# Two-layer graph network: five of the seven products of q, k and v at quarter size, instruction order from tables

## Chip, core and metric

The kernel runs on one core of a Trainium2 chip. The metric is the device time of one execution in microseconds. All data is float32. The core has a matrix engine (TensorE, PE in the profile, with PEld for its weight loads), a vector engine (DVE), an activation engine (ACT), GpSimd (POOL) and a queue that issues transfers (SP). Each of these works through a list of instructions; instructions of different engines are tied together by semaphores. Matrix products are written into eight PSUM banks, from which DVE and ACT take them to SBUF.

## The reference

Two layers over 64 graphs of 256 nodes with 512 features: a graph convolution, then an attention with 8 heads of 64. Cut to what matters:

```python
# x: (64, 256, 512), adj: (256, 256)
h = jnp.maximum(_layernorm(x, axis=-1), 0.0)
x = x + (jnp.einsum('nm,bmd->bnd', adj, h) @ weight + bias)

h = jnp.maximum(_layernorm(x, axis=-1), 0.0)
q = (h @ Wq + bq).reshape(b, n, 8, 64)
k = (h @ Wk + bk).reshape(b, n, 8, 64)
v = (h @ Wv + bv).reshape(b, n, 8, 64)
scores = jnp.einsum('bqhd,bkhd->bhqk', q, k) / 8.0
scores = scores + (1.0 - adj)[None, None, :, :] * -1000000000.0
attn = jax.nn.softmax(scores, axis=-1)
out = jnp.einsum('bhqk,bkhd->bqhd', attn, v).reshape(b, n, d)
x = x + (out @ Wo + bo)
```

The output is x, of shape (64, 256, 512).

## The kernel before

**Groups and layers.** The 64 graphs are taken two at a time: NG = 32 groups of GB = 2. Layer 0 runs over all groups and leaves the residual and the normalised features (transposed) in DRAM. Then layer 1 runs over the groups again. For group g its loop does: attention of the first half of the heads (`attend(g, 0)`), the scores of the second half (`score(g, 1)`), q and k of group g+1 (`queries_keys`), attention of the second half (`attend(g, 1)`), the scores of the first half of group g+1 (`score(g + 1, 0)`), v of group g+1 (`values`), and the output projection of group g (`post`). The o of the last two groups is drawn out at the end.

**Seven products for eight.** Each projection is a 512 by 512 product cut into 2 by 2 blocks, done with seven block products by Strassen's scheme in Winograd's form. With the letters that the change uses: A = a11*b11, B = s3*t3, C = a12*b21, D = a22*t4, E = s4*b22, F = s2*t2, G = s1*t1, where s1 to s4 are sums of weight blocks (`weight_sums`) and t1 to t4 sums of feature blocks (class `Halves`, line 433, written by POOL or DVE at line 450). A, F, G and E are added up in one PSUM bank, pa, from which the four quadrants of the result are taken in between; B and D are added up in pc. A product at the outer level (`product`, line 452) is four instructions with 128 by 128 weights and 256 columns.

**Quarter size.** From group 2 on (FIRST2 = 2) `project2` (line 545) does C, D and E once more by the same scheme: seven instructions with 128 columns each in place of four with 256 (line 568). Their inner sums of features come from the class `Blocks` (lines 541 to 543): three instructions for a Blocks object. Four of the seven (a11*b11, s2*t2, s3*t3, s1*t1 of the inner level) run through a small shared bank: a running total in its first half, which DVE (line 669) or ACT adds into the result after each step, before the next product goes on top of it, and s3*t3 in its second half. The other three go straight into the outer bank. The weights' inner sums are made once by `block_sums` on POOL.

**Order of work.** Each engine runs its instructions in the order in which the program emits them. A counter spreads side work: `after(delay, fn)` enters a piece of work, and `tick()` emits all that has fallen due, by due time and then by entry. The projections are generators; `run` calls `tick()` at each of their yields, seven for a projection. Side work that matters here: the exponentials of a score (line 1009, ACT), the key sums (line 1016, POOL), the sums t1 to t4 of the features of the group after next (`hidden_sums`), their inner sums (`block_hidden`), and the division of the attention (line 1070, DVE). `score` emits 32 matmuls into score banks (line 986), eight DVE instructions that scale and mask them (lines 994 and 997), and for the later two of its four batches a POOL subtraction of the row maximum of the mask (line 1004). Ahead of its matmuls it seeds four banks by ACT (line 259) and emits the inversion of the attention's denominators (lines 1048 to 1052, ACT and POOL).

**Where the inner sums of the features are emitted before.** When v of group g+1 has been emitted, the loop calls `hidden_sums(g + 2, 2, 3, 4, 5)` and `block_hidden(g + 2, 6)`, and then runs o of group g with its seven ticks: the four t sums fall due at ticks 2 to 5, the inner sums of both graphs (`both.sums`) at 6 and those of t4 (`last.sums`) at 7.

**Banks.** `bank()` takes the first free bank of a list (one that holds fresh data everywhere where a seed is to be written, preferably one that does not where `partial` is given) and `give()` puts it at the end.

**Buffers.** `xpool` has four buffers of 1 MB that rotate: in layer 1 for the features of two groups (H1T) and the residuals (X).

Of the kernel before, what the change touches and what calls it, by code (L numbers as in the profile page):

```python
# [196 lines left out]

@with_exitstack
def kernel(
# [37 lines left out]
    xpool = main.enter_context(tc.tile_pool(name="x", bufs=4))  # L237
# [11 lines left out]
    def bank(shape, name, seed=None, times=1.0, partial=False):  # L249

        if seed is not None:
            i = next(i for i in free_banks if whole[i])
        else:
            i = next((i for i in free_banks if not (partial and whole[i])), free_banks[0])
        free_banks.remove(i)
        t = psum.tile(shape, F32, tag=f"bank{i}", name=name)
        bank_of[id(t)] = (i, t)
        if seed is not None:
            nc.scalar.mul(t, seed, times)  # L259
        return t  # L260
# [34 lines left out]
    def load(g):  # L295
        X[g] = xpool.tile([P, T, D], F32, tag="x", name=f"x_{g}")
        for k in range(GB):
            for i in range(NI):
                nc.sync.dma_start(blocks_of(X[g], i, k), by_block(x[g * GB + k], i))
# [133 lines left out]
    class Halves:  # L433

        def __init__(self, name, tokens, which):
            self.tokens = tokens
            self.t = {n: act.tile([P, 2, N], F32, tag=f"{n}{which}", name=f"{n}_{name}")
                      for n in ("t1", "t2", "t3", "t4")}
# [72 lines left out]
    ONCE = {"a12": "b21", "a22": "t4", "s4": "b22"}  # L511
# [3 lines left out]
    def block_sums(n):  # L515

        todo = []
        for a in ONCE:
            w = W[n][a]
# [3 lines left out]
            W2[n, a] = dict(a11=part(0, 0), a12=part(0, 1), a22=part(1, 1), s1=s1, s2=s2, s3=part(1, 0), s4=s4)  # L523
            for o, p, q, op in ((s1, part(1, 0), part(1, 1), ALU.add), (s2, s1, part(0, 0), ALU.subtract),
                                (part(1, 0), part(0, 0), part(1, 0), ALU.subtract), (s4, part(0, 1), s2, ALU.subtract)):
                todo.append((nc.gpsimd.tensor_tensor, o, p, q, op))
        return todo

    class Blocks:

        def __init__(self, x, t):
            self.x, self.t = x, t

# [11 lines left out]
    def project2(n, halves, blocks, by_token, name, place, first, done=None, seeds=(), add_up=False):  # L545

        s = W[n]
# [7 lines left out]
        class Inner:  # L557

            def __init__(self, a, i, k, own, shared):
                self.w, self.x, self.own, self.shared = W2[n, a], blocks[ONCE[a]], own, shared  # L560
                self.sum, self.r = shared[:, 0:1, :], shared[:, 1:2, :]
                self.o = place(i, k)

            def mm(self, o, a, b, start=False):
                lhs, rhs = self.w[a], self.x.operand(b)
                if by_token:
                    lhs, rhs = rhs, lhs
                nc.tensor.matmul(o[:, 0, :], lhs, rhs, start=start, stop=True, skip_group_check=True)  # L568

            def begin(self, src, i, k):  # L570
                first(part(self.o, i, k), src, 0, None if by_token else i)

            def add(self, src, i, k):
                o = part(self.o, i, k)
                add(o, src if src.shape[1] == o.shape[1] else src.to_broadcast([P, o.shape[1], P]), o)

            def u1(self):
                self.mm(self.sum, "a11", "b11", True)

            def only(self, *quarters, fresh=False):  # L580
                for q in quarters:
                    a, b = {(0, 0): ("a12", "b21"), (0, 1): ("s4", "b22"), (1, 0): ("a22", "t4")}[q]
                    self.mm(part(self.own, *q), a, b, fresh)
                    fresh = False

            def u2(self):
                self.mm(self.sum, "s2", "t2")

            def s3t3(self):
                self.mm(self.r, "s3", "t3")  # L590

            def u3(self):
                self.mm(self.sum, "s1", "t1")

        def put(ps, i, k):
            first(place(i, k), ps, i)

        def more(ps, i, k):
            o = place(i, k)
            add(o, ps, o)  # L600

        def complete(i, k):
            if done:
                done(i, k)

        pa, pc = seeds or (bank([P, 2, N], f"{name}a"), None)
        product(pa, s, "a11", halves, "b11", by_token, start=not seeds, stop=False)
        put(pa, 0, 0)
        yield
        pc = pc or bank([P, 2, N], f"{name}c")  # L610
        product(pc, s, "s3", halves, "t3", by_token, start=not seeds, stop=False)
        put(pc, 1, 1)
        yield
        product(pa, s, "s2", halves, "t2", by_token, start=False, stop=False)
        put(pa, 1, 0)
        yield
        inner = []
        for a, i, k, own in (("a12", 0, 0, None), ("a22", 1, 0, pc), ("s4", 0, 1, pa)):
            inner.append(Inner(a, i, k, own, bank([P, 2, P], f"{name}{i}{k}", partial=True)))
            inner[-1].u1()  # L620
        p2, p4, p3 = inner
        for p in inner:
            if p is not p3 or add_up:
                p.add(p.sum, 0, 0)
            else:
                p3.begin(p3.sum, 0, 0)
        p2.own = pb = bank([P, 2, N], f"{name}b", partial=True)
        p2.only((0, 0), (0, 1), (1, 0), fresh=True)

        for m, n in ((0, N), (1, P)) if add_up else ((slice(0, 3), P),):  # L630
            o, u = (t if add_up else t.rearrange("p m (h j) -> p (m h) j", j=P) for t in (p2.o, pb))
            add(o[:, m, 0:n], u[:, m, 0:n], o[:, m, 0:n])
        give(pb, False)
        yield
        product(pa, s, "s1", halves, "t1", by_token, start=False, stop=False)
        more(pa, 1, 1)
        complete(1, 1)
        yield
        for p in inner:
            p.u2()  # L640
            p.s3t3()
            if p is not p3 or add_up:
                p.add(p.sum, 1, 0)
                p.add(p.r, 1, None)
            else:
                p3.begin(p3.sum, 1, 0)
                p3.begin(p3.r, 1, 1)
                p3.add(p3.r, 1, 0)
        yield
        p4.only((0, 0), (0, 1), (1, 0))  # L650
        p3.only((0, 1), (0, 0), (1, 0))
        more(pc, 1, 0)
        give(pc)
        if add_up:
            more(pa, 0, 1)
        else:
            p3.begin(part(pa, 0, 1), 0, 1)
            p3.add(part(pa, 0, 0), 0, 0)
            p3.add(part(pa, 1, None), 1, None)
        give(pa)  # L660
        for p, c in zip(inner, ((0, 0), (1, 0), (0, 1))):
            p.u3()
            p.add(p.sum, None, 1)
            give(p.shared, False)
            complete(*c)
        yield
# [193 lines left out]
    def load_hidden(g):  # L860
        H1T[g] = xpool.tile([P, GB, DC, N], F32, tag="x", name=f"h1T_{g}")
# [4 lines left out]
    def load_residual(g):  # L866
        X[g] = xpool.tile([P, T, D], F32, tag="x", name=f"x1_{g}")
        nc.sync.dma_start(X[g], X1[g].rearrange("k (t p) d -> p (k t) d", p=P))

    def hidden_sums(g, *steps):  # L870

        HH[g] = Halves(f"h_{g}", [H1T[g][:, k] for k in range(GB)], 0 if g else 1)
        for step, n in zip(steps, ("t3", "t1", "t2", "t4")):
# [3 lines left out]

    def block_hidden(g, step):

        t = act.tile([P, GB, 4, P], F32, tag="t2", name=f"t2_{g}")  # L880
        t4 = act.tile([P, 4, P], F32, tag="t24", name=f"t24_{g}")
        x = H1T[g][:, :, 2:4, :].rearrange("p k c (n j) -> p k c n j", j=P)
        H2[g] = block_sums_of(x, t, HH[g], t4, nc.gpsimd, step)

    def block_outputs(g, eng, step):
# [4 lines left out]
        else:  # L890
            t4 = act.tile([P, 4, P], F32, tag="t24", name=f"t24o_{g}")
            t = act.tile([P, GB, 4, P], F32, tag="t2", name=f"t2o_{g}")
        O2[g] = block_sums_of(x, t, HO[g], t4, eng, step)

    def block_sums_of(x, t, halves, t4, eng, step):
        both = Blocks(x, t)
        last = Blocks(halves.t["t4"].rearrange("p c (n j) -> p c n j", j=P), t4)
        after(step, both.sums, eng)
        after(step + 1, last.sums, eng)
        return {"b21": Blocks(x[:, 0], t[:, 0]), "b22": Blocks(x[:, 1], t[:, 1]), "t4": last}  # L900

    def queries_keys(g):

        for n, store in (("q", Q), ("k", K)):
            store[g] = {}
            bias = L1[n][1]

            def first(o, ps, i, m=None):
                for c in range(2) if m is None else (m,):
                    to, src = (o[:, c, :], ps[:, c, :]) if m is None else (o, ps)  # L910
                    nc.scalar.activation(to, src, AF.Identity, bias=bias[:, 2 * i + c:2 * i + c + 1])

            def place(i, k):
# [4 lines left out]
            if g < FIRST2:  # L918
                yield from project(W[n], HH[g], False, f"{n}_{g}", place, first)
            else:  # L920
                yield from project2(n, HH[g], H2[g], False, f"{n}_{g}", place, first)

    def values(g):
# [3 lines left out]
        def first(o, ps, i, m=None):  # L927
            nc.scalar.copy(o, ps)

        def place(i, k):  # L930
            return V[g][i, k]

        if g < FIRST2:
            yield from project(W["v"], HH.pop(g), True, f"v_{g}", place, first)
        else:
# [307 lines left out]
```

## Time and profile before

| | us |
|---|---|
| median of 3 runs | 2659.88 (2659.43 to 2661.59) |
| profiled execution, its own time | 2660.27 |
| its span in the trace | 2658.5 |
| scores (line 986) on PE | 240.2 in 2048 records |
| attention (line 1032) on PE | 233.6 in 4096 records |
| key sums (line 1016) on POOL | 319.6 in 256, 1.275 each |
| mask subtractions (line 1004) on POOL | 292.7 in 125, 2.363 each |
| POOL idle before the inversion (line 1050), for ACT | 452.8 in all |

A float32 matmul leaves two records on PE, so an instruction is two of the records that the profile counts. Times of records overlap, since matmuls are pipelined: what an instruction costs is read from the distance of starts. A line that ends in x8 is eight records in a row, and the number behind "idle" in a timeline is the time in which the engine stood still ahead of the instruction, with what ended it.

### The profile page before, as it was taken

How to read it: one execution, taken by the hardware profiler on the slowest of the kernel's cores; microseconds unless marked ns; L12 is line 12 of the kernel's file. 1: busy time of each engine (PE TensorE's matmuls, PEld its weight loads, DVE VectorE, ACT ScalarE, POOL GpSimd, SP SyncE). 2: the span in 40 equal slices, each digit the busy share in tenths (PEclk: the TensorE clock that was granted, in tenths of full speed). 3: DMA queues.
4: the chain of work that ended last, by engine and by line, in shares of the span. 5: the costliest groups of instructions: out<-in, count | busy, mean ns of one | idle time of the engine just before them, and what ended most of it. 6: DMA issues, size and time to landing. Idle time of an engine off the chain costs nothing. (4 is left out here: it accounts for less than half of the span.)

```text
span 2658.5 us, 52085 instructions
## 1 busy us (share of the span) xinstructions
PE 2623.4 (99%) x20076; PEld 2283.1 (86%) x20076; DVE 1648.6 (62%) x3613; ACT 1144.4 (43%) x2194; POOL 1883.9 (71%) x1899
## 2 busy tenths in 40 slices
PE   7999999999999999999999999999999999999997
PEld 6999899998888888888888888888888888888886
DVE  5878888884355555556556555556556555555556
ACT  3445454443344444444444444444444444444442
POOL 5888888774677776666677777777777776666665
PEclk9999999999999999999999999999999999999999
DMA  5776666665022211111111111111222211111110
GB/s 135 200 192 188 171 167 171 178 157 125 28 62 54 51 48 49 49 49 49 49 49 48 49 48 49 49 49 49 60 63 64 55 49 49 49 48 49 49 49 34
DMA packets 281068, 211.06 MB, mean 79 GB/s; under 512 B 145904, under 2 KB 212976, under 8 KB 280816
## 3 DMA queue, kind: packets, MB, share of 16 engines
q1 hardware_dynamic: 280352, 207.15, 29.9%
q8 instruction: 161, 2.64, 0.4%
q14 instruction: 91, 0.75, 0.1%
q10 hardware_dynamic: 464, 0.52, 0.1%
HBM read 106.96 MB, written 100.66 MB: 78 GB/s over the span
## 5 line engine op out<-in xcount | busy, mean ns | idle before, releaser
L1050 POOL TENSOR_TENSOR rest<-rest 128x512 f32<-128x512 f32 x63 | 80.1, 1271 | 452.8 <-ACT rest L1049 452.8
L1016 POOL TENSOR_TENSOR as<-a 128x512 f32<-128x512 f32 x256 | 319.6, 1275 | 57.4 <-ACT a L1009 57.4
L1004 POOL TENSOR_TENSOR a<-a,top 128x1024 f32<-128x1024 f32 x125 | 292.7, 2363 | 57.2 <-DVE a L997 57.2
L994 DVE SCALAR_TENSOR_TENSOR a<-sc,top 128x512 f32<-128x512 f32 x256 | 159.1, 684 | 276.4 <-PE sc L986 276.3
L1009 ACT ACTIVATE a<-a 128x1024 f32<-128x1024 f32 x256 | 270.8, 1059 | 4.3 <-DVE a L1002 3.1
L986 PE MATMUL sc<-q,k 64*128 64x256 f32 x2048 | 240.2, 383 | 1.4 <-ACT sc L259 1.4
L986 PEld LDWEIGHTS sc<-q,k 64*128 64x128 f32 x2048 | 196.9, 186 | 45.3 <-ACT rest L1048 25.9
L1032 PE MATMUL pav<-a,v 128*32 128x256 f32 x4096 | 233.6, 379 | 0.0
L1041 ACT ACTIVATE rest<-pden 128x512 f32<-128x512 f32 x64 | 38.2, 597 | 413.9 <-PE pden L1025 413.9
L1032 PEld LDWEIGHTS pav<-a,v 128*32 128x32 f32 x4096 | 133.3, 110 | 88.0
L42 DVE BATCH_NORM_STATS2 st<-x 128x6 f32<-128x512 f32 x256 | 173.1, 676 | 10.7 <-DMA x<-in_x_dram 8.5
L669 DVE TENSOR_TENSOR k<-k,k 128x128 f32<-128x128 f32 (+1 forms) x300 | 96.1, 353 | 126.5 <-PE k L568 124.1
L997 DVE SCALAR_TENSOR_TENSOR a<-sc,maskT 128x512 f32<-128x512 f32 x256 | 158.3, 680 | 0.0
L259 ACT ACTIVATE sc<-maskT 128x512 f32<-128x512 f32 x256 | 137.5, 591 | 0.0
L669 DVE TENSOR_TENSOR q<-q,q 128x128 f32<-128x128 f32 (+1 forms) x300 | 96.2, 353 | 65.9 <-PE q L568 63.5
L669 DVE TENSOR_TENSOR v<-v,v 128x128 f32<-128x128 f32 (+1 forms) x300 | 95.5, 351 | 65.2 <-PE v L568 62.1
L697 ACT ACTIVATE h<-x,nb,rs 128x512 f32<-128x512 f32 x128 | 93.9, 803 | 75.8 <-POOL nb L54 73.4
L824 ACT ACTIVATE h<-x,nb,rs 128x512 f32<-128x512 f32 x128 | 97.2, 807 | 52.3 <-POOL nb L54 49.1
L669 DVE TENSOR_TENSOR x<-o,x 128x128 f32<-128x128 f32 (+1 forms) x360 | 111.0, 350 | 3.1
L758 POOL TENSOR_TENSOR hs<-h 128x512 f32<-128x512 f32 x31 | 39.3, 1269 | 73.8 <-ACT h L697 63.7
L450 POOL TENSOR_TENSOR t_o<-oT,t_o 128x512 f32<-128x512 f32 x62 | 79.1, 1276 | 13.0 <-DVE t_o L450 10.6
L450 POOL TENSOR_TENSOR t_y<-yT 128x512 f32<-128x512 f32 (+1 forms) x65 | 82.2, 1265 | 5.9 <-ACT yT L808 5.9
(4817 smaller groups left out, 7302.6 us busy)
## 6 DMA issues: line engine op xcount, KB each, us to landing
x<-in_x_dram SPq DMA_DIRECT2D x256, 128.0 KB, 3.0
residual<-x SPq DMA_DIRECT2D x256, 128.0 KB, 2.5
hidden<-r SPq DMA_DIRECT2D x128, 256.0 KB, 4.5
h1T<-hidden SPq DMA_DIRECT2D x64, 512.0 KB, 9.6
x<-residual SPq DMA_DIRECT2D x32, 1024.0 KB, 7.6
out_dram<-x SPq DMA_DIRECT2D x62, 512.0 KB, 4.0
w_sb<-in_L_gnn_weight_dram SPq DMA_DIRECT2D x1, 1024.0 KB, 8.2
wq_sb<-in_L_gnn_Wq_dram SPq DMA_DIRECT2D x1, 1024.0 KB, 7.9
```

The lines of the kernel that those rows point to most:

```text
L42: nc.vector.bn_stats(st, src)
L259: nc.scalar.mul(t, seed, times)
L450: eng.tensor_tensor(self.t[n][:, c, :], self.operand(p, c), self.operand(q, c), op=ALU.subtract)
L669: nc.vector.tensor_tensor(o, ps, u, op=ALU.add)
L824: nc.scalar.activation(h1[:, k * NT + t, :], xt[:, k * NT + t, :], AF.Relu, bias=nb[:, t:t + 1], scale=rs[:, t:t + 1])
L986: nc.tensor.matmul(ps[j][:, kt * N:(kt + 1) * N], k[j * HD:(j + 1) * HD, c, kt * P:(kt + 1) * P], q[j * HD:(j + 1) * HD, c, :], start=(kt ...
L994: nc.vector.scalar_tensor_tensor(o, ps[j].rearrange("p (k n) -> p k n", k=NT), SCALE, top_b[:, 0:NT, :], op0=ALU.mult, op1=ALU.subtract)
L997: nc.vector.scalar_tensor_tensor(o.rearrange("p k n -> p (k n)"), ps[j], SCALE, maskT_f, op0=ALU.mult, op1=ALU.add)
L1004: nc.gpsimd.tensor_tensor(a, a, top_b, op=ALU.subtract)
L1009: nc.scalar.activation(a, a, AF.Exp)
L1016: nc.gpsimd.tensor_tensor(AS[c, b], a4[:, :, 0, :], a4[:, :, 1, :], op=ALU.add)
L1032: nc.tensor.matmul(po[f][h * 32:(h + 1) * 32, b * N:(b + 1) * N], v[:, k, h * HD + f * 32:h * HD + f * 32 + 32], A[h // 2, b][:, (h % 2) * ...
```

## The change

F and G join C, D and E for q, k and v: five of their seven products are now done at quarter size. o keeps C, D and E. F and G cannot add their inner sums into the four result quadrants, as they belong into the running total pa. So the running totals are copied from the small bank to a staging tile in SBUF by ACT, three copies a product (`staged`: b, e and g), DVE adds s3*t3 (h), the three direct products go into pa (i, j, k), and DVE adds the whole staging tile into pa (l).

`project2` goes away. `quartered` builds a dictionary of named steps, one for each instruction or so, and `follow` emits them in the order of a table, where "|" is a yield (a tick) and "x" the next exponential of the score before. A token is the projection (q, k, v, o), the product (A to G) and a letter or number; p and m are the takings of a quadrant from pa or pc, and z is a seed. QK interleaves q and k, VO interleaves v of group g+1 and o of group g, and V1, O1 and OL are for v or o alone: V1 in the turns of g = 1 and g = 30, O1 and OL for the o of the last two groups.

Further parts: the inner sums of the features now cover t1, t2 and t4 (`last` is a Blocks object over all three at once, in a tile kept in the fourth buffer of xpool); t3 is written over b12 (in layer 0 too); the sums of the group after next are entered by `multiplied`, when the last matmul of v has been emitted, with delays 1 to 4, 5 and 6; exponentials of the scores between the tables are not entered with a delay but taken by "x", with the key sum one tick later; the buffers of xpool have fixed tags, so the residual has one (x2), and its load is entered four ticks later; the inner sums of the weights for F and G are made on DVE, k's at ticks 16 and on in group 0.

The tables that the loop uses for most groups, and the core of the diff:

```diff
+QK = (
+    "kFa qA0 kFb qFa kGa qFb qA1 x qA2 | qGa kFc kFd kA0 kFe x kA1 | kFf kA2 kFg qA3 kFh kA3 qp000 | qFc qp001 "
+    "qFd qDa kp000 qB0 qFe qB1 kp001 | x qB2 kFl qFf qFi qFj qFg qFk qGb kB0 qFh | kB1 qFl x qGc qGd kB2 qGe kDa "
+    "kGb | qp100 kFi qGf qp101 kGc kGd qGg kFj qDb kGe kFk qGh qB3 | kp100 qGl qDc kp101 qDd qCi qp110 qDe qCj "
+    "kDb qCk qp111 qDf kGi | kGj qCl kDc kDd qGi kDe qGj kDf qGk kEa qm11 | kGk kEb kGf kDg kGg qDi kDh kEc kEd "
+    "kGh qDj kEe kGl qCa | kCa kEf kB3 qCb kCb qDg kEf2 kp110 qCc qDh qCd kp111 kEg | qCe kCc qCf kCd qEa km11 "
+    "kDi qEb qCg kDj kCe qCh kDk | qEc kCf kEi km10 qEd kEj qEe kCi kCj qEf kCk | kCg qEf2 qDk kCl qEi qEj kCh "
+    "qEk qm10 qEg qEl0 kEk | kEl1 qEh kEl0 qEl1 qEl2 kEl2 kEh ")
+VO = (
+    "vFa oBz vA0 vFb vA1 oAz vFc vFd x vGa | vA2 vB0 vGb vB1 vFe x vB2 | vFf vGc vEa vFg vGd vEb vA3 vFh vGe oA0 "
+    "| vp00 vEc vGf vCa vFl vGg vDa oA1 x vCb vGh | oA2 oA3 vFi op00 vCc vCd vEd | vCe vFj x vCf vFk vCi vCj vCk "
+    "vCg vp10 vCl oB0 | vEe oB1 vCh vEf vDb vGi vEf2 oB2 vGl vDc vDd | vB3 vDe vDf oCa vp11 oCi oCb vGj vGk vDg | "
+    "vm11 vDi vDj vDk vDh oCj oCk vm10 vEi vEj oCl0 | vEk oDa vEl0 vEg oCl1 oF0 vEl1 vEl2 oF1 vEh oF2 | oEa oF3 "
+    "oEb oB3 op10 oEc | oEd oDb oCc op11 oCd oG0 oCe oG1 oCf oEe oG2 | oEf oG3 oDi om11 oDc oDd oEg | oDe oCg oDf "
+    "oDj oDk oEh oEi oCh oEj oEk om10 oDg | oEl oDh ")
...
-                      for n in ("t1", "t2", "t3", "t4")}
+            self.all = act.tile([P, 3, 2, N], F32, tag=f"t{which}", name=f"t_{name}")
+            self.t = {n: self.all[:, i] for i, n in enumerate(("t1", "t2", "t4"))}
+            self.t["t3"] = self.operand("b12")
...
+    SMALL = {"q": "CDEFG", "k": "CDEFG", "v": "CDEFG", "o": "CDE"}
...
+        def sums(x, names):
+            t = x + "s"
+            for name, a, b, i in zip(names, ("a11", "s2", "s3", "s1"), ("b11", "t2", "t3", "t1"), (0, 0, 1, 0)):
+                multiply(x, name, a, b, t, i, None, dict(partial=True) if a == "a11" else None)
+            return t, lambda: banks[t][:, 0:1, :], lambda: banks[t][:, 1:2, :]
+
+        def staged(x, b):
+
+            t, total, rest = sums(x, "acdf")
+            held = {}
+
+            def copy(name, c):
+                def todo():
+                    if not held:
+                        held[0] = act.tile([P, 2, 2, P], F32, tag="stage", name=f"{n}_{g}_{x}", bufs=2)
+                    o = held[0][:, c[0], c[1], :] if len(c) == 2 else held[0][:, :, 1, :]
+                    nc.scalar.copy(o, total()[:, 0, :] if len(c) == 2 else total().to_broadcast([P, 2, P]))
+                step(x + name, todo, t)
+
+            def add_rest():
+                o = held[0][:, 1]
+                add(o, rest().to_broadcast([P, 2, P]), o)
+
+            def add_all():
+                u = held[0].rearrange("p k i j -> p i k j") if by_token else held[0]
+                o = banks[b].rearrange("p m (h j) -> p m h j", j=P)
+                add(o, o, u)
+            copy("b", (0, 0))
+            copy("e", (1, 0))
+            copy("g", (1,))
+            step(x + "h", add_rest, t)
+            last_three(x, "ijk", b)
+            step(x + "l", add_all, b)
+
+        def added(x, to, quadrant=None, begin=False):
+
+            t, total, rest = sums(x, "acdg")
+
+            def put_in(name, src, i, k):
+                step(x + name, lambda: first(part(to(), i, k), src(), quadrant[0], i), t, quadrant=quadrant)
+
+            def add_in(name, src, i, k):
+                def todo():
+                    o = part(to(), i, k)
+                    add(o, like(o, src()), o)
+                step(x + name, todo, t, quadrant=quadrant)
+            if begin:
+                put_in("b", total, 0, 0)
+                put_in("e", total, 1, 0)
+                put_in("f", rest, 1, 1)
+                add_in("f2", rest, 1, 0)
             else:
...
+                add_in("b", total, 0, 0)
+                add_in("e", total, 1, 0)
+                add_in("f", rest, 1, None)
+            add_in("h", total, None, 1)
...
+        product("A", "pa", True)
+        put("p00", "pa", 0, 0)
+        product("B", "pc", True)
+        put("p11", "pc", 1, 1)
+        for x, name, end, i in (("F", "p10", put, 0), ("G", "m11", more, 1)):
+            if x in SMALL[n]:
+                staged(x, "pa")
+            else:
+                product(x, "pa", False)
+            end(name, "pa", 1, i)
...
+    def follow(steps, order):
+
+        for token in order.split():
+            if token == "|":
+                yield
+            elif token == "x":
+                if exponents:
+                    next_exponent()
+            else:
+                steps.pop(token)()
+        assert not steps, steps.keys()
...
+        both = Blocks(H1T[g][:, :, 2:4, :].rearrange("p k c (n j) -> p k c n j", j=P), t)
+        last = Blocks(HH[g].all.rearrange("p t c (n j) -> p t c n j", j=P), kept[0])
+        after(step, both.sums, nc.gpsimd)
+        after(step + 1, last.sums, nc.gpsimd)
+        H2[g] = {"C": both.one(0), "E": both.one(1), "G": last.one(0), "F": last.one(1), "D": last.one(2)}
...
+                if exps is None:
+                    exponents.append((a, g, qd, c, b))
+                else:
+                    after(exps[2 * c + b], exponent, a)
+                    after(sum_delay + 2 * c + b, key_sum, g, qd, c, b)
...
+    def next_exponent():
+        a, *which = exponents.pop(0)
+        exponent(a)
+        after(1, key_sum, *which)
...
-            steps = values(g + 1)
-            run(steps, 5)
-            seeds = seed_outputs(g) if g + 2 < NG else None
-            run(steps)
-            if g + 2 < NG:
-                hidden_sums(g + 2, 2, 3, 4, 5)
-                if g + 2 >= FIRST2:
-                    block_hidden(g + 2, 6)
-                run(post(g, seeds))
+
+            def multiplied(g=g):
+                del HH[g + 1]
+                H2.pop(g + 1, None)
+                if g + 2 < NG:
+                    hidden_sums(g + 2, 1, 2, 3, 4)
+                    if g + 2 >= FIRST2:
+                        block_hidden(g + 2, 5)
+
+            n, halves, *rest = values(g + 1)
+            if g + 1 < FIRST2:
+                run(plain(g + 1, n, halves, *rest))
+                multiplied()
+            else:
+                steps = quartered(g + 1, n, halves, H2[g + 1], *rest, multiplied=multiplied)
+                if FIRST2 <= g < NG - 2:
+                    steps.update(quartered_outputs(g))
+                    run(follow(steps, VO))
+                else:
+                    run(follow(steps, V1))
+            if g < FIRST2:
+                run(plain_outputs(g))
```

## The prediction

> **What bounds the kernel now.** I read the page first, its busy rows and slices. The chain of waits is no help here: it has one piece, a 0.33 us add at the very end.
>
> ```profile
> span 2658.5 us, 52085 instructions
> PE 2623.4 (99%) x20076; PEld 2283.1 (86%) x20076; DVE 1648.6 (62%) x3613; ACT 1144.4 (43%) x2194; POOL 1883.9 (71%) x1899
> PE   7999999999999999999999999999999999999997
> PEclk9999999999999999999999999999999999999999
> ```
>
> TensorE is the bound, at a full granted clock, and the list of its waits names under 30 us in all; in the windows from 750 to 2500 us it is busy throughout. So less TensorE work is worth its whole length, and any wait put into its queue costs its whole length too. Next the window of one group, from the first matmul of q of group 14 to that of group 15:
>
> ```profile
> 1490.06:1553.07 63.01, 63.01 (x522) 54.35 (x520) 36.68 (x86) 26.73 (x55) 44.12 (x39) 1.00 0.20 52
> ```
>
> (PE, PEld, DVE, ACT, POOL busy us.) TensorE has no gap in 63.01 us; the others have 26, 36 and 19 us to spare. Then the timeline of TensorE, for the two prices that the change trades:
>
> ```profile
> 1491.89 1.89 PE L457 MATMUL q_14c<-t_h,wq_sb 128*128 128x256 f32 x8
> 1493.62 1.89 PE L457 MATMUL q_14a<-t_h,wq_s 128*128 128x256 f32 x8
> ...
> 1498.41 0.38 PE L568 MATMUL q<-t,spare_w_sb 128*128 128x128 f32 x2
> 1498.63 0.39 PE L568 MATMUL q<-t,wq_sb 128*128 128x128 f32 x2
> ...
> 1499.75 0.39 PE L568 MATMUL q_14c<-t_h,wq_sb 128*128 128x128 f32 x2
> ```
>
> A plain product (8 records, 4 instructions) goes on after 1.73 us (1491.89 to 1493.62), 0.432 us an instruction. A quarter-size instruction (2 records) goes on after 0.223 us: six of them between 1498.41 and 1499.75. Seven make 1.563 us.
>
> Last the timelines of POOL and DVE where attention ends and q begins. In this group q's first matmul starts at 1553.07, which I call S.
>
> ```profile
> 1548.94 0.73 POOL L541 TENSOR_TENSOR t<-t_h 128x256 f32<-128x256 f32 x1
> 1549.75 0.46 POOL L542 TENSOR_TENSOR t<-t_h,t 128x128 f32<-128x128 f32 x1
> 1550.29 0.46 POOL L543 TENSOR_TENSOR t<-t_h,t 128x128 f32<-128x128 f32 x1
> 1550.70 1.27 POOL L1050 TENSOR_TENSOR rest<-rest 128x512 f32<-128x512 f32 x1
> ...
> 1552.76 1.27 POOL L1052 TENSOR_TENSOR rest<-rest 128x512 f32<-128x512 f32 x1
> 1554.43 4.68 POOL L1004 TENSOR_TENSOR a<-a,top 128x1024 f32<-128x1024 f32 x2 [0.40 <-DVE a L997]
> 1559.08 1.27 POOL L450 TENSOR_TENSOR t_o<-oT 128x512 f32<-128x512 f32 x1
> ```
>
> ```profile
> 1553.07 2.47 DVE L997 SCALAR_TENSOR_TENSOR a<-sc,maskT 128x512 f32<-128x512 f32 x4
> 1555.47 1.28 DVE L1070 TENSOR_TENSOR oT<-pav,rest 128x512 f32<-128x512 f32 x2
> ```
>
> Two things to see. The inner sums of the hidden features (L541 to L543) are finished at 1550.75, just ahead of the inversion and the two mask subtractions (L1004), which hold POOL until S+6.0. And DVE empties the last score banks well after TensorE has left the scores: its L997 rows end at S+0.68, +1.28, +1.87 and +2.47.
>
> **What is removed.** In q, k and v of groups 2 to 31 two plain products (s2*t2, called F, and s1*t1, called G) become seven quarter-size instructions each: 1.73 - 1.563 = 0.167 us less. 30 groups x 3 projections x 2 = 180 products: 30.1 us off TensorE. The product o keeps its three.
> The trace has fp32 quarter-size records 0.112 us apart. [...]
>
> **What is moved, and costs most.** The inner sums of group g+2 are emitted by the tick counter. Before, they are entered after v has ended and due at 6 and 7, with the seven ticks of o still to come, so all stand on POOL before the next attention. Now they are entered by `multiplied`, when the last matmul of v in the table VO (vEg) is issued. Behind vEg stand five bars, so five ticks: t1, t3, t2, t4 and the sums of both tokens go out at 1 to 5, but `last.sums`, due at 6, falls to the tick behind the next score. In POOL's queue it now stands behind the inversion and the two L1004 subtractions of that score, where L450 stands today: S+6.0. It has also grown from one half-sum to three (t1, t2, t4 at once). No row has 768 and 384 elements; L541 to L543 and L450 show 0.46, 0.73 and 1.27 us for 128, 256 and 512, that is 2.1 ns an element, so 1.81 and 1.00 us (bounds from the nearest rows: 0.73 and 0.46 below, the 1024 row's 2.36 and 1.27 above). The second result (sub-sum t2) is there at 6.01 + 1.81 + 0.08 + 1.00 = S+8.90, with 0.07 us for the signal (the gap seen from pden's end to ACT's read) S+8.97.
> The table QK wants it early: ahead of kFc, which multiplies by that t2, stand kFa, qFa, kGa and qGa (4 x 0.223) and qA0 to qA2 (3 x 0.432), 2.19 us. TensorE takes matmuls in order, so it waits 8.97 - 2.19 = 6.78 us a group, with everything of q and k behind it. Bounds: 5.2 us (POOL 1.27 in all) to 7.6 us (3.71). Groups 4 to 31 get their sums this way: 28 x 6.78 = 189.8 us. Groups 2 and 3 do not, since there the seven ticks of a plain o follow.
> On whether POOL could go round the waiting instructions: its row at 1554.43 shows 0.40 us of idling for DVE with later work due. [...]
>
> **Banks.** I walked the list of free PSUM banks through a group. At the start of VO and of QK it holds, in order, the last six score banks and the two of the attention. VO takes the second for a seed and the third (free at S+0.68, with the signal 0.75) for vA0, which is reached at 0.22: 0.53 us a group (bounds 0 and twice that), 28 x 0.53 = 14.8 us. In QK kGa takes the fourth (1.35 against 0.88): 0.47 us, swallowed by the wait for the sums except in groups 2 and 3, 0.9 us.
>
> **What costs nothing, and its cover.** Per group ACT gets 18 staging copies (12 x 0.26 + 6 x 0.37 = 5.3 us, rows of 128 elements and of q's puts) on 26.7 of 63 us. DVE gets 6 x (0.36 + 0.68) = 6.2 us of adds, on 36.7. The tables put two to six other matmuls between a sum, its copy and the next accumulation; uncovered, DVE's part alone would be 187 us. The four exponentials of a score leave the tick counter for the x of the tables, and each key sum follows a tick later; on POOL they stand behind `last.sums` and t_o (1.27) and end near S+17 (4 x 1.25), which the next attention reads at S+29. POOL idles 14.75 us ahead of the next L1050 today, so the 3.9 us more are covered. t3 overwriting b12 adds no instruction. The residual has one buffer and is loaded four ticks later: it lands 7.6 us after its issue, some 20 us before o reads it; on SP only the stores of o stand behind it. The 24 extra block sums of weights on DVE (0.3 us each) run once, in group 0 and 1. The last two o follow tables of their own; TensorE has 15 us idle in the last 159 us today, and I take 0, bounds -5 and +5.
>
> **The sum.** 2658.5 - 30.1 + 189.8 + 14.8 + 0.9 = 2833.9 us of span. The profiled execution took 2660.27, 1.8 above its span, and the median of the runs is 0.4 below it: 2835.3, forecast 2835 (0.72). Own range: 2774 (low sums, no bank wait) to 2873.
>
> **Rivals.** (a) The sums are there in time and TensorE keeps its gain (0.17): -30.1 + 14.8 + 30 x 0.47 gives 2657 of span if the bank waits stay, 2628 if they do not; some 2644 timed. For it: the tables start q and k with F and G, which only makes sense with ready sums, and POOL has 19 us to spare. Against: the tick count and POOL's order. It decides if last.sums starts ahead of S - 0.7, so that kFc finds it.
> (b) The wait is there, and the staging is not covered either (0.11): in the middle of QK and VO my walk finds 0 or 1 bank free, so each of eight inner banks a table waits for a DVE add just done. If half of them cost one add of 0.5 us, 2 us a table, 58 tables: 2835 + 116 = 2951. Against: DVE is at 58% in the window. It decides once TensorE idles over 0.1 us before the inner sums D, C and E.
>
> **Range and chances.** A measurement of this kernel can tell some 0.2% from no change, 5.3 us. Faster 0.15 and same 0.02 are (a); slower 0.83 is the forecast and (b). For 8 in 10 the range runs from 2774 to 2930, into (b).
>
> **What would show it.** In the changed profile: a wait of PE for POOL's block sums, 28 times, 6 to 7 us each, soon after the scores; L1004 and then the 768-element sum on POOL; plain products gone from 16 to 8 instructions a projection; a group of about 69.3 us (63.01 - 1.00 + 6.78 + 0.53). A group below 63 us, or inner sums ahead of the inversion, makes it wrong.

## The result and the profile after

The changed kernel takes 2914.22 us (median of 6 runs, 2912.58 to 2917.32) against 2661.40 for the kernel before, measured again beside it (6 runs, 2659.43 to 2662.15). The ratio is 1.0952, 95% interval 1.0938 to 1.0966: 9.5% slower. The forecast of 2835 us has the direction and the mechanism, and 79 us too little of it.

The page of the changed kernel: span, busy time by engine, two rows of the slices, and two of the costliest groups (out<-in, busy and mean ns, then the idle time of the engine ahead of them and what ended most of it).

```profile
span 2915.3 us, 54495 instructions
PE 2696.9 (93%) x21156; PEld 2355.3 (81%) x21156; DVE 1853.3 (64%) x4000; ACT 1291.2 (44%) x2742; POOL 1951.3 (67%) x1896
PEclk9999999999999999999999999999999999999999
L631 PE MATMUL k_Fs<-spare,spare 128*128 128x128 f32 x120 | 41.6, 449 | 167.9 <-POOL spare L579 167.9
L645 PE MATMUL k_pa<-h1T,wk_sb 128*128 128x256 f32 x240 | 105.6, 563 | 0.0
```

TensorE was busy 99% of the time and is now busy 93%. One group of instructions has nearly all of the new idle time: the matmul of k's F that reads the second inner sum, 167.9 us, released by POOL. The last row is easy to pass over: the plain product A of k waited for nothing, and yet a record of it takes 563 ns on average, where the same form takes 380 ns in o. The row of the granted clock can't explain that: a 9 there stands for everything from 0.9 up.

The list of TensorE's waits (what waits, for what; us in total, times, longest) leaves no doubt which wait it is.

```profile
PE k_Fs L631 <- POOL spare L579: 167.9, 28, 6.0
PE pa L365 <- DVE adj_p L360: 9.9, 1, 9.9
PE v_pa L645 <- DVE a L1101: 6.9, 28, 0.2
PE o_Ds L631 <- POOL t_o L481: 5.6, 1, 5.6
```

28 times is the forecast's own count: groups 4 to 31. Here is POOL in one of them (start, duration, instruction). q and k begin at S = 1657.56.

```profile
1656.75 1.27 POOL L1164 TENSOR_TENSOR rest<-rest 128x512 f32<-128x512 f32 x1
1658.91 4.66 POOL L1108 TENSOR_TENSOR a<-a,top 128x1024 f32<-128x1024 f32 x2 [0.89 <-DVE a L1101]
1663.53 1.81 POOL L578 TENSOR_TENSOR spare<-t_h 128x768 f32<-128x768 f32 x1
1665.41 0.99 POOL L579 TENSOR_TENSOR spare<-t_h,spare 128x384 f32<-128x384 f32 x1
1666.48 1.00 POOL L580 TENSOR_TENSOR spare<-t_h,spare 128x384 f32<-128x384 f32 x1
```

After the end of the inversion (L1164) come the two mask subtractions, and the inner sums stand behind both. TensorE in the same stretch:

```profile
1657.56 0.49 PE L631 MATMUL k_Fs<-t_h,wk_s 128*128 128x128 f32 x2
...
1660.08 0.38 PE L631 MATMUL q_Gs<-t_h,wq_s 128*128 128x128 f32 x2
1666.46 0.80 PE L631 MATMUL k_Fs<-spare,spare 128*128 128x128 f32 x2 [5.99 <-POOL spare L579]
1667.47 1.91 PE L645 MATMUL k_pa<-h1T,wk_sb 128*128 128x256 f32 x4
1671.77 0.38 PE L631 MATMUL q_Fs<-spare,spare 128*128 128x128 f32 x2
```

The waiting matmul starts at S + 8.90. The list says 6.0 us for the wait, but it counts from the end of the matmul ahead, which itself had been held up a little by a bank. Against an unhindered stream the loss is 8.90 - 2.19 = 6.71 us. And it does not end there. The two instructions at 1666.46 and 1667.47 show 0.80 us for two records and 1.91 for four, against 0.38 and 1.03 before the wait. The windows of the same stretch (us; busy time and instructions of PE, PEld, DVE, ACT and POOL; granted clock of TensorE; DMA share and GB/s) say why:

```profile
1662.00:1664.00 2.00, 0.00 (x0) 0.00 (x0) 0.00 (x0) 0.00 (x0) 2.00 (x2) 1.00 0.27 103
1664.00:1666.00 2.00, 0.00 (x0) 0.00 (x0) 0.00 (x0) 0.00 (x0) 1.92 (x2) 0.63 0.00 0
1666.00:1668.00 2.00, 1.54 (x6) 1.45 (x7) 0.00 (x0) 0.28 (x2) 1.92 (x3) 0.50 0.00 0
1668.00:1670.00 2.00, 2.00 (x7) 1.68 (x6) 0.00 (x0) 1.09 (x2) 2.00 (x3) 0.50 0.00 0
1670.00:1672.00 2.00, 2.00 (x9) 1.65 (x8) 0.42 (x1) 0.69 (x3) 1.16 (x1) 0.67 0.00 0
1672.00:1674.00 2.00, 2.00 (x15) 1.84 (x14) 0.69 (x1) 2.00 (x6) 0.00 (x0) 1.00 0.00 0
```

The granted clock falls to one half at 1664.51, 4.4 us after the last matmul started, and is back at 1671.34. Of these 6.83 us 1.95 lie in the wait. In the other 4.88 TensorE works at half speed and loses 2.44 us. So a group costs, first the group ahead as a whole, then this one in its two halves:

```profile
1585.88:1657.56 71.68, 65.32 (x559) 56.66 (x557) 43.02 (x99) 31.61 (x73) 46.39 (x39) 0.95 0.16 43
1657.56:1697.54 39.98, 33.88 (x286) 29.31 (x285) 21.13 (x49) 18.56 (x45) 17.80 (x14) 0.91 0.14 39
1697.54:1729.24 31.70, 31.45 (x275) 27.33 (x273) 21.90 (x51) 13.16 (x28) 28.59 (x26) 1.00 0.22 56
```

71.68 us against 63.01. The half with v and o (31.70, before 31.51) is the shorter v (-0.33, worked out from the prediction's rows) and a bank wait of 0.52. The half with q and k (39.98, before 31.51) is -0.67 for the shorter products (worked out in the same way), 6.71 for the wait and 2.43 that remain, about the 2.44 of the half clock. From group 2 to group 31 that makes 235.9 us of the 256.8 that the span has grown by. The start has 7.2 (up to the q of group 2), the end 13.7, of which 8.5 are one more such group.

### The profile page after: what moved, and what is told of

The parts are those of the page before. It is cut to its first block, busy times and chain, and to the rows that moved or that the text cites. A ratio compares the mean times of both kernels' runs of the same rounds, so it can differ in the third digit from the quotient of the medians.

```text
span 2915.3 us, 54495 instructions
## 1 busy us (share of the span) xinstructions
PE 2696.9 (93%) x21156; PEld 2355.3 (81%) x21156; DVE 1853.3 (64%) x4000; ACT 1291.2 (44%) x2742; POOL 1951.3 (67%) x1896
## 5 line engine op out<-in xcount | busy, mean ns | idle before, releaser
L1162 POOL TENSOR_TENSOR rest<-rest 128x512 f32<-128x512 f32 x63 | 80.1, 1272 | 575.0 <-ACT rest L1161 575.0
L1108 POOL TENSOR_TENSOR a<-a,top 128x1024 f32<-128x1024 f32 x125 | 292.6, 2364 | 70.4 <-DVE a L1101 70.4
L631 PE MATMUL k_Fs<-spare,spare 128*128 128x128 f32 x120 | 41.6, 449 | 167.9 <-POOL spare L579 167.9
L668 ACT COPY k_F<-k_Fs 128x128 f32<-128x128 f32 (+1 forms) x90 | 27.1, 301 | 345.6 <-PE k_Fs L631 345.6
L631 PEld LDWEIGHTS k_Fs<-spare,spare 128*128 128x128 f32 x120 | 34.2, 315 | 178.4 <-POOL spare L579 173.2
L772 DVE TENSOR_TENSOR k_F<-k_Fs,k_F 128x256 f32<-128x256 f32 x30 | 12.7, 425 | 255.3 <-ACT k_F L668 255.3
L645 PE MATMUL o_pa<-wo_s,t_o 128*128 128x256 f32 x480 | 118.8, 380 | 0.0
L772 DVE TENSOR_TENSOR x<-o_pa,x 128x512 f32<-128x512 f32 x120 | 82.7, 689 | 38.2 <-PE o_pa L645 23.7
L645 PE MATMUL k_pa<-h1T,wk_sb 128*128 128x256 f32 x240 | 105.6, 563 | 0.0
```

What stands on the lines that cost most here:

```text
L645: nc.tensor.matmul(t[:, m, :], lhs, rhs, start=starts, stop=True, skip_group_check=True)
L772: nc.vector.tensor_tensor(o, ps, u, op=ALU.add)
L1108: nc.gpsimd.tensor_tensor(a, a, top_b, op=ALU.subtract)
```

## The experiments

The theory was that the order on POOL, nothing else, makes TensorE wait, and that a clock that falls in the wait makes up what the forecast lacks. The rivals were that the products at quarter size and their staging cost time of their own, and that the lateness costs something by another way than through the early reading. "Before" is run beside each kernel, 2659.9 to 2660.7 us.

**The inner sums ahead of the attention.** One tick earlier, and `last.sums` is emitted ahead of the next score.

```diff
-                        block_hidden(g + 2, 5)
+                        block_hidden(g + 2, 4)
```

> The inner sums fall due one tick earlier, so all of them stand on POOL ahead of the attention and the scores. My theory (late sums, 6.71 us of waiting a group, and 2.48 us of half clock after it, in 28 groups): both go, the bank waits of 0.36 us in VO and 0.47 us in QK stay, a group takes about 62.84 us and the kernel about 2667 us; no PE wait for POOL in the middle. Rival (staging not covered): a group stays 2 us or more above that and the kernel at 2725 or higher. Rival (the order tables cost nothing once the sums are in time): 2644 or lower.

2669.88 us, ratio 1.0040 (1.0025 to 1.0054). The wait for POOL is gone from the list, and one group, from the first matmul of a denominator (pden, two in a group) to the next but one, is

```profile
1520.96:1584.00 63.04, 62.69 (x557) 54.73 (x556) 43.08 (x98) 31.61 (x74) 46.26 (x38) 1.00 0.19 51
```

So one tick is worth 244 us. It also answers the rival on staging: every copy and every add is still there, and TensorE stands still for 0.35 us of 63.04. What is left is not a gain either, since the quarter-size products (-0.94 a group, by the last experiment) are paid back by bank waits: without them, in the last experiment, the half with v is 0.51 shorter (31.18 for 31.69) and the half with q and k 0.46 (30.89 for 31.35).

**The wait kept, the clock held up.** The kernel as changed, with 13 matmuls of spare operands into a free bank ahead of the waiting matmul from the third table QK on; their result is not used.

```diff
...
+            if token == "kFc":
+                fills.append(0)
+                if len(fills) > 2:
+                    fill()
```

> The sums stay late, but 13 matmuls of 256 columns whose result nobody reads (5.6 us) are issued ahead of kFc in groups 4 to 31, so that TensorE is busy while it waits. If the half clock comes from the idling: the clock stays at 1.00 and 2.48 us a group come back, 28 x 2.48 = 69 us, about 2845 us. If the half clock has another cause (or is a fixed price of the late sums): about 2914 us, as the changed kernel. If the matmuls of no use are not hidden by the wait: above 2914.

2847.99 us (one time). The list of waits and the window of one group:

```profile
PE k_Fs L631 <- POOL spare L579: 11.4, 28, 0.4
```

```profile
1518.68:1588.01 69.33, 68.57 (x583) 59.59 (x582) 42.99 (x98) 31.51 (x74) 46.39 (x38) 1.00 0.18 47
```

The waiting matmul still starts at S + 8.93, so nothing is sooner, but TensorE has something to do until then, the clock stays at 1.00, and the group takes 69.33 us: the forecast's 69.3. The 66 us between this kernel and the changed one are the clock alone (28 x 2.35).

**The same lateness in the kernel before.** Its `block_hidden` gets one tick more, so that the inner sums of t4 are emitted after the score.

```diff
-                    block_hidden(g + 2, 6)
+                    block_hidden(g + 2, 7)
```

> The kernel before with its inner sums of t4 put behind the next score (due one tick later). The result t2 would be there at 6.01 + 0.73 + 0.08 + 0.46 = 7.28 us after the start of q, and the kernel before reads it only at about 8.7 us. My theory: no wait, 2661 us within 0.2%. If lateness on POOL alone costs: some us a group, 2700 or more.

2659.31 us, ratio 0.9999 (0.9990 to 1.0009). The sums do stand behind the subtractions in its trace: in the group whose q begins at 1551.96, the second result is there at S + 7.27, and the first matmul of D that reads it starts at S + 8.80. They are shorter there than in the changed kernel, and so 1.6 us less late. A sum that is late costs nothing where it is read later still. It takes both, the late sum and a table that begins with it.

**The lateness kept, the table begun with A and B.** These two plain products of q and of k need no inner sums; they go to the front, F and G behind them.

```diff
-    "kFa qA0 kFb qFa kGa qFb qA1 x qA2 | qGa kFc kFd kA0 kFe x kA1 | ...
+    "qA0 qA1 qA2 qA3 qp000 kA0 qp001 kA1 kA2 kA3 kp000 qB0 kp001 qB1 qB2 qB3 qp110 kB0 qp111 kB1 kB2 kB3 "
+    "kp110 kp111 kFa kFb qFa kGa qFb x | qGa kFc kFd kFe x | ...
```

> The sums stay late, but QK issues the products A and B of q and k first (16 x 0.432 = 6.9 us), F and G after them. My theory: kFc is reached at 7.8 us after the start instead of 2.2, so 1.1 us of waiting stay instead of 6.7, the clock does not fall, the bank waits at the start of QK go: a group of about 63.6 us, 2690 us. If lateness on POOL itself, and not the early reading of the sums, sets the time: near 2914.

2783.21 us (one time), 93 above what was expected. The long wait is gone, but four others have come.

```profile
PE k_Fs L631 <- POOL spare L579: 24.3, 28, 0.9
PE q_Ds L631 <- DVE k_F L772: 22.3, 30, 0.7
PE k_Fs L631 <- ACT k_F L668: 11.5, 32, 0.5
PE q_Cs L631 <- DVE q L772: 6.2, 30, 0.2
```

A and B had been the matmuls that stand between an inner product, its copy and the next one. Taken away from there, they leave TensorE waiting for ACT's copies (L668) and DVE's adds (L772): the second rival of the prediction, which the changed kernel does not show, is real as soon as its cover is gone. The waits of the list make 64 us of the 113 above the kernel with sums ahead (2669.88), 24 of them still for the late sums. The granted clock has a mean of 0.992, against 0.996 there: in nine groups it falls to one half for 3.41 us, which costs at most 15 us in all, though no wait in these groups is longer than 0.9 us. The other 34 us were not taken apart.

**The sums behind the inversion, ahead of the subtractions.** `last` is kept in a list (`pending`) and its sums are emitted within the score, where `score` has emitted the inversion.

```diff
+        if g >= FIRST2 + 2:
+            pending.append(last)
...
+        while pending:
+            pending.pop(0).sums(nc.gpsimd)
```

> The inner sums of t1, t2 and t4 are emitted inside the score, on POOL behind the inversion and ahead of the two mask subtractions, in groups 4 to 31. My theory: t2 is there 3.9 us after the start of q, 1.74 us of waiting a group, too short for the clock to fall: a group of 64.1 us, 2914 - 28 x 7.57 = 2702 us, clock 1.00. If any wait costs half clock: 2740 or more.

2693.22 us (one time). That is 0.83 us a group above the kernel with the sums ahead (23.3 / 28). In the trace a group takes 63.78 us, 0.74 above, and the waiting matmul starts at S + 3.38 (expected 3.9) against S + 2.74 with the sums ahead. The clock is 1.00 in the window from 1300 to 1500 us:

```profile
PE k_Fs L631 <- POOL spare L579: 13.2, 28, 0.5
```

**The sums between the two subtractions.** The same loop over `pending`, after the first L1108.

> The same sums between the two mask subtractions. t2 is there 6.6 us after the start of q: 4.4 us of waiting, about 4.0 us of idle TensorE. With the clock unhurt: a group of 66.8 us, 2778 us. [...]

2829.70 us (one time), 52 above the figure for an unhurt clock; the mean clock is 0.978.

```profile
PE k_Fs L631 <- POOL spare L579: 103.5, 28, 3.7
```

The wait is 2.3 us shorter a group than in the changed kernel (64 us in all), and the clock is still lost, in all 28 groups: for 3.41 us in 24 of them, for 6.83 in four. In the group shown it goes down even after TensorE has begun again, at 2108.51 us (timeline of TensorE, then windows):

```profile
2104.43 0.38 PE L631 MATMUL q_Gs<-t_h,wq_s 128*128 128x128 f32 x2
2108.51 0.49 PE L631 MATMUL k_Fs<-spare,spare 128*128 128x128 f32 x2 [3.69 <-POOL spare L579]
```

```profile
2106.50:2108.50 2.00, 0.00 (x0) 0.00 (x0) 0.00 (x0) 0.00 (x0) 1.88 (x2) 1.00 0.31 120
2108.50:2110.50 2.00, 1.99 (x8) 1.73 (x9) 0.00 (x0) 1.22 (x2) 1.97 (x2) 0.65 0.00 0
2110.50:2112.50 2.00, 2.00 (x7) 1.64 (x7) 0.42 (x1) 0.37 (x1) 2.00 (x2) 0.50 0.00 0
2112.50:2114.50 2.00, 2.00 (x14) 1.84 (x13) 0.00 (x0) 1.61 (x6) 2.00 (x3) 0.99 0.00 0
```

The whole wait passes at 1.00, and the fall comes at 2109.12; the half clock lies in the work behind it. Against the kernel with the sums ahead this one is 159.8 us slower, 5.7 a group, of which the list of waits knows only 3.7. The waiting matmul starts 3.9 us later (S + 6.60 for S + 2.74), and most of the rest is the half clock.

**F and G as plain products again**, on top of the sums ahead: the kernel computes with the products of the kernel before, but in the order of the tables.

```diff
...
-    SMALL = {"q": "CDEFG", "k": "CDEFG", "v": "CDEFG", "o": "CDE"}
+    SMALL = {"q": "CDE", "k": "CDE", "v": "CDE", "o": "CDE"}
```

> The sums ahead of the scores, the same tables, but F and G of q, k and v as plain products again (no staging copies, no adds of the staging tile, four 256-column matmuls for seven quarter-size ones). If the quartering saves what its rows say and the staging is covered: a group 1.00 us longer than without bank waits, that is 63.0 us as before, and, as the tables then ask for no bank early, no bank waits: about 2670 + 30 - 25 = 2675 us. If the staging costs as much as the quartering saves: 2645 or lower.

2676.18 us, ratio 1.0059 (1.0042 to 1.0076), group 63.15 us. This is +0.11 us against 63.04 with F and G at quarter size: with the sums in time, the change's main idea is worth next to nothing as placed, since what it saves goes into bank waits.

**Banks.** The sums ahead, and A moved to where a bank is free: the openings of both tables.

```diff
-    "kFa qA0 kFb qFa kGa qFb qA1 x qA2 | qGa
+    "kFa qA0 kFb qA1 qFa x qA2 kGa qFb | qGa
...
-    "vFa oBz vA0 vFb vA1 oAz vFc vFd x vGa | vA2 vB0
+    "vA0 vFa vA1 vFb oBz vA2 oAz vFc vFd x vGa | vB0
```

> The sums ahead of the scores, and at the start of QK and VO the first matmuls reordered so that no bank is asked for before DVE has emptied it (F of q and G of k after two more matmuls of A, the seeds of o behind v's first four matmuls). My theory of the bank waits: 0.47 us in QK and 0.36 us in VO go in 28 to 30 groups, a group takes about 62.0 us (63.01 less 1.00 of quartering), the kernel 2670 - 28 x 0.83 = 2647 us. If the gaps at the start have another cause: 2670 us.

2650.87 us, ratio 0.9964 (0.9952 to 0.9977), group 62.42 us: 0.46 less in the half with q and k, 0.17 in that with v, where the bank wait has moved on to vB0, 0.24 us. POOL's timeline, with the sums where they belong, done ahead of the inversion (L1162 to L1164):

```profile
1546.61 1.83 POOL L578 TENSOR_TENSOR spare<-t_h 128x768 f32<-128x768 f32 x1
1548.52 1.00 POOL L579 TENSOR_TENSOR spare<-t_h,spare 128x384 f32<-128x384 f32 x1
1549.59 1.00 POOL L580 TENSOR_TENSOR spare<-t_h,spare 128x384 f32<-128x384 f32 x1
1550.55 1.28 POOL L1162 TENSOR_TENSOR rest<-rest 128x512 f32<-128x512 f32 x1
```

**All together.** In addition vA3 goes ahead of vB0, the table O1 begins with A and B, and the seeds of the first o are written after the fifth step of v.

```diff
-    "... oAz vFc vFd x vGa | vB0 ... vEb vA3 vFh ...
+    "... oAz vFc vFd x vGa vA3 | vB0 ... vEb vFh ...
-    "oDa oAz oCi oCj oCk oBz oA0 oA1 x | oA2 oA3 oB0 x oB1 | ...
+    "oAz oBz oA0 oA1 oA2 oA3 | op00 oB0 oB1 oB2 oB3 | ...
...
+                run(steps, 5)
+                seeds = seed_outputs(g)
+                run(steps)
```

> Sums ahead of the scores and banks asked for in the order in which DVE empties them, as in the run with the reordered starts (2651 us), and three more edits. One more matmul of v's A ahead of v's first B, which asked for a bank 0.24 us too early: 28 x 0.24 = 6.7 us. The order of o of group 30 begins with A, B and C's direct products in place of D and C's, whose sums came 5.6 and 2.2 us late with half clock after them: 6 to 12 us. The seeds of the first plain o are written while v still runs: 2.2 us of waiting and 2 us of half clock. By my theory 2651 - 17 to -25, some 2630 us, under the kernel before by about 1.1%. If the waits of the end and of the start lie beside other waits: 2640 to 2651.

2642.87 us, ratio 0.9934 (0.9920 to 0.9947), the fastest of all. One group and two of the waits that are left:

```profile
1507.64:1569.71 62.07, 62.07 (x557) 54.60 (x556) 42.99 (x98) 31.22 (x74) 46.28 (x38) 1.00 0.19 52
```

```profile
PE o_Ds L631 <- DVE x L772: 5.5, 1, 5.5
PE o_pa L645 <- DVE x L772: 3.4, 2, 2.6
```

TensorE has no gap in the group, and 63.01 - 62.07 = 0.94 us is what the quarter-size products bring. It is 13 us above the 2630 of the theory, and inside the range named for waits that lie beside others, because the o of group 30 still waits: its D for DVE, 5.5 us, where it had waited 5.6 for POOL. The new table only changed what is late there. A group that is 0.94 shorter would give 28 us over 30 groups; 18 are measured, and the end and the start keep the rest.

## Why the prediction was right, and what it left out

**Right, by the numbers.** `last.sums` stood behind the inversion and the two subtractions, as the count of ticks said, and its rows took 1.81, 0.99 and 1.00 us (worked out: 1.81 and 1.00). The waiting matmul started at S + 8.90 (8.97) and the wait was worth 6.71 us (6.78) in 28 groups (28). Only the experiments show that this order is the cause: one tick earlier removes it, the lateness without the early reading costs nothing. The bank wait of the half with v was 0.52 us (0.53), and that of the half with q and k, which the wait swallows, appears as 0.46 (0.47) once the sums are in time. The gain in products was 0.94 us a group (1.00).

**Rival (a)**, the sums in time with the bank waits kept, is what the kernel with the sums ahead measures: 2669.9 against 2657 + 1.8, the difference being the start and the end below. **Rival (b)**, staging uncovered, did not come in the changed kernel; the kernel with A and B in front shows that its mechanism exists.

**The step that failed** is the price of the wait: "28 x 6.78 = 189.8 us" charges a wait with its length alone. The wait also brings the clock down, and the work behind it runs at half speed for 4.88 us: 28 x 2.43 = 68 us (66 by the kernel with filling matmuls), missing from the sum. The prediction had read the granted clock, found it full and treated it as given, while its own forecast made TensorE idle for over six us in each group. Nothing in the trace before had such a stall in its loop, so the size could not be read there, but the question could have been put. The kernel with filling matmuls shows the term by itself: with the wait at full length and the clock at 1.00 the group is 69.33 us, and the time 2848 is within 13 us of the forecast, which are the start and the end below. The sum's own range ended at 2873, so 2914 lies outside it. That the wider range took it in is luck: its upper part, to 2930, was there for rival (b), which did not come.

**Also failed, and smaller:** "The last two o follow tables of their own [...] I take 0, bounds -5 and +5". The end costs 5.2 us beyond the last group's wait and half clock (13.7 - 8.5), for O1 begins with D, whose operands POOL has not made:

```profile
2870.12 0.80 PE L631 MATMUL o_Ds<-wo_sb,t_o 128*128 128x128 f32 x2 [5.60 <-POOL t_o L481]
2873.94 0.79 PE L631 MATMUL o_pb<-wo_sb,rest 128*128 128x128 f32 x2 [2.17 <-POOL rest L580]
```

The start costs 7.2, of which some 4 are the first o, whose seeds are written only after v (a wait of 2.2 us and a lower clock behind it); the other 3 are in the first layer, which ends between 646.9 and 650.7 us in the traces here, whatever the kernel, so that they may be no effect of the change. Clock, start and end make 68 + 7.2 + 5.2 = 80.4 of the 81.4 us by which the span is above the forecast's 2833.9.

## What to carry to other kernels

Where one engine is the bound, ask of every piece of side work not only when it is emitted but what stands ahead of it in its queue and how early the table on the other side reads it; here one tick in a counter was worth 244 us. Price a stall of TensorE as its length plus what the clock then costs (here 6.71 and 2.43 us a group), and if a stall of some us in a loop can't be avoided, give TensorE something to do: matmuls of no use took 66 us off this kernel. A change that saves TensorE instructions in a kernel with full banks also has to say which bank each new first write takes, for here the bank waits equalled the saving (0.51 and 0.46 us a group against 0.94).

## What the runs showed of the hardware

**When the clock fell.** In the changed kernel it fell at 947.71, 1019.39 and 1664.51 us. 1664.51 - 947.71 = 716.80 us = 210 x 3.4133, and times at half clock in this trace are 3.41 us (719.02 to 722.43), 6.83 (1664.51 to 1671.34) and 10.24 (2869.42 to 2879.66). All 33 falls of this trace, from 29.53 to 2913.79 us, lie whole multiples of that step apart. The period of the groups, 72.00 and 71.84 us at first, settled at 71.68 = 21 x 3.4133. With the sums between the subtractions it is no such multiple (68.84 us on average between 938.24 and 2521.53, 20.2 steps), and yet its falls at 1556.16, 1764.37, 2109.12 and 2313.92 are 208.21, 344.75 and 204.80 us apart, 61, 101 and 60 steps. The one at 2109.12 came 0.61 us behind the end of the wait (2108.51), the one at 2313.92 0.49 us ahead of it (2314.41): there the moments of the falls keep to the step, not to the wait.

**What cost the clock.** Windows of one step that meet at a fall show it. Two are of the changed kernel, two of the one with the sums between the subtractions, two of the one that begins with A and B:

```profile
1661.10:1664.51 3.41, 0.00 (x0) 0.00 (x0) 0.13 (x1) 0.00 (x0) 3.41 (x3) 1.00 0.43 162
1664.51:1667.92 3.41, 1.46 (x6) 1.37 (x7) 0.00 (x0) 0.20 (x2) 3.25 (x4) 0.50 0.00 0
```

```profile
2105.70:2109.12 3.42, 0.61 (x5) 0.61 (x6) 0.00 (x0) 0.00 (x0) 3.26 (x3) 1.00 0.43 165
2109.12:2112.53 3.41, 3.41 (x11) 2.79 (x11) 0.42 (x1) 1.60 (x3) 3.41 (x3) 0.50 0.00 0
```

```profile
1550.40:1553.81 3.41, 1.97 (x12) 1.59 (x13) 0.76 (x2) 3.07 (x6) 3.33 (x4) 1.00 0.00 0
1553.81:1557.22 3.41, 3.41 (x18) 3.41 (x17) 1.49 (x3) 2.39 (x7) 3.41 (x4) 0.50 0.00 0
```

The first of each pair has a full clock and little TensorE work, the second half the clock. With the trace of the changed kernel divided into such windows from 26.11 us on, half the clock followed on every window at full clock with 1.37 us or less of TensorE busy, 33 times, and on none with 1.72 or more. The last pair, of the other kernel, has it behind 1.97 us, so between 1.72 and 1.97 these traces show both. In the changed kernel the clock came back behind windows at half clock with 3.41 us busy and stayed at half behind those with 2.31 or less; none lies between. So the length of one stall does not say what it costs. A stall of 0.5 us a group left the clock at 1.00 (the sums behind the inversion), one of 3.7 us cost it in each group (the sums between the subtractions), and stalls of at most 0.9 us cost it where together they left 1.44 us of one window idle (the last pair).

**The first matmul behind a wait** took 0.49 us for its two records, the ones that follow 0.39, at full clock too (0.49 and 0.39 at 2108.51 and 2108.83, with the sums between the subtractions): some 0.1 us on top of a wait. The first matmul of k behind the scores of the changed kernel shows 0.49 at 1657.56 as well, with no idle time ahead of it, so it is not shown that the wait itself is the reason.
